# Transposes as products of column quarters with the identity, and one row a head of the row sums, in a two-layer graph network

## The chip, the cores and the metric

The kernel runs on one core of one Trainium2 chip. The metric is the device time of an execution in microseconds. The kernel before took 3508.07 us, the median of three runs (3501.76 to 3508.48).

## The reference

Sixteen graphs (B = 16) of N = 1024 nodes with D = 256 features are sent through two layers with one adjacency matrix a graph (int32, 1024 x 1024). All is f32. Cut to what matters:

```
h = relu(layernorm(x));  n = layernorm(h) * gamma1 + beta1            # layer 0
q = n as 8 heads of 32
a = softmax(where(adj > 0, q q^T / sqrt(32), -inf));  h = h + a q
h = h + gelu((layernorm(h) * gamma2 + beta2) W1 + b1) W2 + b2;  x = x + h
f = relu(layernorm(x));  u = f W                                       # layer 1
l = leaky_relu(u a_1 + (u a_2)^T + u a_12 u^T);  a = softmax(where(adj > 0, l, -9e15))
x = x + elu(f W_1 + (a f) W_2)
```

## The kernel before, in words

`fast_path` computes it when a bound on gamma1 and beta1 holds; `general_path` below it isn't entered here. Nodes lie on the 128 partitions in 8 tiles per graph (NT = 8), and each graph goes through these stages:

- `prologue` (lines 753 to 860) loads x, makes h and the values va, and its `turn` (796) transposes va into kT with features on partitions: 16 transposes of 128 x 128 per graph, four per call (two tiles of nodes, two groups of heads), into one PSUM tile `ptk` (801), copied by ScalarE (804).
- `attention` (931) has 32 units per graph: 2 halves of 512 queries, 2 groups of 4 heads (GH = 4), 8 key tiles. A unit makes `s`, the scores of four heads, in four row strips of the array (950, 32*128 in the profile), adds the mask on VectorE (971), takes exp on ScalarE (974), and a unit later `weigh` (982) makes `o` in four column strips, 32 columns a head (987). Sums of the exps are gathered by DMA (1011). `total` (896) turns them into `den` (901), where the sum of a head stands in all of that head's 32 rows, and copies it to `ds`.
- `finish` (914) transposes `ds` (row sums) and `os` (unnormalized outputs), four transposes each (922) into `ptds` and `ptos`, takes the reciprocal of one column a head of `ptds` (925), multiplies (927), and GpSimd adds it into h.
- `rest` (1074) has the feed-forward part and layer 1: `turn` (1107) transposes y into `pty` (1117); `expand` makes `ph` (1137), `contract` makes `po` (1160); `turn1` (1187) transposes the features into `ptf` (1193); `project` makes `puT`, `values` makes `pg`, `weights` the logits `lg`, read by VectorE (1241), `own` makes `pf`, and `attend` (1265) makes `pa`.

Those last products go through `matmul` (565): it cuts a product with 128 output rows into four with 32 columns of the stationary operand each ("quarters"), while the flag `quarters[0]` is set. The flag is cleared in `close_attention` (1048), after the last unit of attention, so that the last graph's rest of the work is on the whole array. The transposes don't go through it.

Graphs overlap: `stream_a` (attention of graph b), `stream_b` (rest of graph b - 1), `stream_c` (prologue of graph b + 1) and others are merged by places written out by hand (1446 to 1451), with a `clock` that counts planned us and `defer` for work that is due later. The order on each engine is fixed to the order of the program (1467 to 1476). Transposes are queued in `turns`, and `make_turns` (885) runs them ahead of a unit's scores, when there is room among three PSUM tiles (`psm`, tag `ps`): one tile for ptk, pty and ptf, two for finish. So a block of four transposes stands, mostly, after a quarter product or `o`, and before `s`. `setup` (660) transposes one weight once (672).

Of the kernel before, what the change touches and what calls it, by code (L numbers as in the profile page):

```python
# [9 lines left out]
F32 = mybir.dt.float32  # L10
# [6 lines left out]
P = 128  # L17
# [476 lines left out]
def fast_path(  # L494
# [28 lines left out]
    nc = tc.nc  # L523
    B, N, D = x.shape
    DFF = W1.shape[1]
    H, HD = 8, D // 8
    GH = 4
# [6 lines left out]
    TPH = QW // P  # L534
    CW = 256
    NCH = N // CW
    TPC = CW // P
# [3 lines left out]
    const = pool("const", 1)  # L541
# [16 lines left out]
    def ps_tile(shape, name, dtype=F32):  # L558
        return psm.tile(shape, dtype, tag="ps", name=name)
# [3 lines left out]
    quarters = [True]  # L563

    def matmul(out, lhsT, rhs, start=True, stop=True):
        if not quarters[0]:
            nc.tensor.matmul(out, lhsT, rhs, start=start, stop=stop)  # L567
            return
        for c in range(0, P, HD):
            nc.tensor.matmul(out[c : c + HD], lhsT[:, c : c + HD], rhs, start=start, stop=stop)  # L570

# [21 lines left out]

    ident = const.tile([P, P], F32, name="ident")
    make_identity(nc, ident)
    ident8 = const.tile([P, P], FP8, name="ident8")
    nc.vector.tensor_copy(ident8, ident, saturate=False)  # L600
    ones = const.tile([P, HD], F32, name="ones")
# [58 lines left out]
    def setup():  # L660
        wl, wa, wT, wb = (lp1.tile([P, DC, D], F32, tag="e1", name=f"stage_{i}") for i in range(4))
        weights_to_load.extend([(wl, W), (wa, a_12)])
        for t, src in rows_to_load:
            nc.sync.dma_start(t, src)
        for t, src in weights_to_load:
            nc.scalar.dma_start(t, src.rearrange("(c p) n -> p c n", p=P))
        yield

        for oc in range(DC):
            pt = ps_tile([P, DC, P], f"p_wT_{oc}")  # L670
            for ic in range(DC):
                nc.tensor.transpose(pt[:, ic, :], wl[:, ic, oc * P : (oc + 1) * P], ident)
            nc.scalar.copy(wT[:, oc, :], pt.rearrange("p c q -> p (c q)"))
        clock[0] += 0.5
        yield

        def product(dst, lhs, rhs, n, name):

            for oc in range(DC):
                pp = ps_tile([P, n], f"p_{name}_{oc}")  # L680
                for kc in range(DC):
                    matmul(
                        pp,
                        lhs[:, kc, oc * P : (oc + 1) * P],
                        rhs[:, kc, :n],
                        start=(kc == 0),
                        stop=(kc == DC - 1),
                    )
                nc.scalar.copy(dst[:, oc, :], pp)

        product(wb, wa, wT, D, "wb")
        clock[0] += 1.7
        yield
        product(wm, wT, wb, D, "wm")
        product(w_a2.unsqueeze(2), wT, a2c.unsqueeze(2), 1, "w_a2")
        product(wo2[:, :, D : D + 1], wT, a1c.unsqueeze(2), 1, "w_a1")
        nc.gpsimd.memset(wo2[:, :, D + 1 : D + 2], 0.0)
        clock[0] += 2.0
        yield


        sq = lp1.tile([P, DC * D], F32, tag="e1", name="sq")
        few = smallp.tile([P, 2 * DC], F32, tag="few", bufs=1, name="few")
        wmf = wm.rearrange("p c n -> p (c n)")
        nc.vector.tensor_tensor(sq, wmf, wmf, op=ALU.mult)
        nc.vector.tensor_tensor(few[:, :DC], w_a2, w_a2, op=ALU.mult)
        nc.vector.tensor_tensor(few[:, DC:], wo2[:, :, D], wo2[:, :, D], op=ALU.mult)
        nc.vector.tensor_reduce(seen[:, 0:1], sq, axis=mybir.AxisListType.X, op=ALU.add)
        nc.vector.tensor_reduce(seen[:, 1:2], few, axis=mybir.AxisListType.X, op=ALU.add)
        yield  # L710
# [25 lines left out]
    def defer(us, f):  # L736
        deferred.append((clock[0] + us, len(deferred), f))

        return clock[0] + us

    def run_deferred(until=0.0):
        while True:
            due = [d for d in deferred if d[0] <= max(until, clock[0])]
            if not due:
                return
            d = min(due, key=lambda d: d[:2])
            deferred.remove(d)
            d[2]()
# [4 lines left out]
    def prologue(b, st):  # L753
# [3 lines left out]
        va = st["va"] = vp.tile([P, NT, D], F32, tag="va", name=f"va_{b}")  # L757
# [38 lines left out]
        def turn(i):  # L796
            clock[0] += 0.5
            pt = ps_tile([P, NG, CW], f"ptk_{b}_{i}")
            for g in range(NG):
                for j in range(TPC):  # L800
                    nc.tensor.transpose(  # L801
                        pt[:, g, j * P : (j + 1) * P], va[:, i * TPC + j, g * P : (g + 1) * P], ident
                    )
            nc.scalar.copy(kT[:, :, i * CW : (i + 1) * CW], pt)

        steps = [
# [4 lines left out]
            value,  # L811
            lambda i: None,
            lambda i: turns.append((1, lambda: turn(i))),
        ]
        if b == 0:
# [25 lines left out]
            measure(1, "b")  # L841
            value(0)
            turn(0)
            convert(2)
            value(1)
            turn(1)
            convert(3)
            for f in (lambda i: measure(i, "a"), rectify, lambda i: measure(i, "b"), value):
# [65 lines left out]
    def finish(b, qh, g, ds, os):  # L914
        h = hs[b]
        finished[b, qh] = finished.get((b, qh), 0) + 1
        clock[0] += 1.0
        pts = []
        for n, c in (("ds", ds), ("os", os)):
            pt = ps_tile([P, TPH, P], f"pt{n}_{b}_{g}_{qh}")  # L920
            for t in range(TPH):
                nc.tensor.transpose(pt[:, t, :], c[:, t * P : (t + 1) * P], ident)  # L922
            pts.append(pt.rearrange("p t (j d) -> p t j d", d=HD))
        rl = smallp.tile([P, TPH, GH], F32, tag="rl", name=f"rl_{b}_{g}_{qh}")
        nc.vector.reciprocal(rl, pts[0][:, :, :, 0])
        ot = tmpp.tile([P, TPH, GH, HD], F32, tag="w2", bufs=3, name=f"ot_{b}_{g}_{qh}")
        nc.vector.tensor_mul(ot, pts[1], rl.unsqueeze(3).to_broadcast([P, TPH, GH, HD]))
        ho = h[qh][:, :, g * P : (g + 1) * P]
        nc.gpsimd.tensor_add(ho, ho, ot.rearrange("p t j d -> p t (j d)"))

# [143 lines left out]
    def rest(b, st, tails):  # L1074
# [10 lines left out]
        def add_residuals(t):  # L1085
            ht = h[t // TPH][:, t % TPH, :]
            nc.gpsimd.tensor_add(ht, ht, b2r)
            nc.gpsimd.tensor_add(xt[t], xt[t], ht)
# [4 lines left out]
        def ask(turn, c):  # L1093

            def f():
                clock[0] += 0.5
                turn(c)
                turned.add((turn, c))
            turns.append((1, f))
            if not quarters[0]:  # L1100
                make_turns()
# [5 lines left out]
        def turn(c):  # L1107
            if st["y", c][1] is not None:
                run_deferred(st["y", c][1])
            y = st["y", c][0]  # L1110
            for i in range(TPC):
                defer(4.0 * i + 2.0, lambda t=c * TPC + i: add_residuals(t))
            yT[c] = tmpp.tile([P, DC, CW], F32, tag="yT", name=f"yT_{b}_{c}")
            pt = ps_tile([P, DC, CW], f"pty_{b}_{c}")
            for dc in range(DC):
                for i in range(TPC):
                    nc.tensor.transpose(  # L1117
                        pt[:, dc, i * P : (i + 1) * P], y[:, i, dc * P : (dc + 1) * P], ident
                    )
            for dc in range(DC):  # L1120
                nc.vector.tensor_scalar(
                    yT[c][:, dc, :],
                    pt[:, dc, :],
                    g2[:, dc : dc + 1],
                    be2[:, dc : dc + 1],
                    op0=ALU.mult,
                    op1=ALU.add,
                )
# [46 lines left out]
        ft, ready1 = {}, {}  # L1175
# [11 lines left out]
        def turn1(c):  # L1187
            run_deferred(ready1[c])
            fT = st["fT"]
            pt = ps_tile([P, DC, CW], f"ptf_{b}_{c}")  # L1190
            for i in range(TPC):
                for dc in range(DC):
                    nc.tensor.transpose(  # L1193
                        pt[:, dc, i * P : (i + 1) * P], ft[c][:, i, dc * P : (dc + 1) * P], ident
                    )
            nc.scalar.activation(fT[:, :, c * CW : (c + 1) * CW], pt, AF.Relu)

        def project(qh, oc, fT, uT):
# [242 lines left out]
    def stream_s():  # L1441
        yield -0.3
        for i, _ in enumerate(setup()):
            yield 0.25 + 0.05 * i
# [3 lines left out]
    while any(p is not None for p in places):  # L1448
        i = min((p, i) for i, p in enumerate(places) if p is not None)[1]
# [92 lines left out]
```

## Time and profile before

| | |
|---|---|
| timed runs | 3508.48, 3508.07, 3501.76 us |
| the profiled execution | 3501.46 us, span 3499.6 us |
| TensorE clock granted | 0.998 |
| PE busy | 3445.0 us (98%), 46590 matmul records |
| DVE, ACT, POOL busy | 2758.3, 1857.8, 1412.8 us |
| transposes ptk, pty, ptf, ptds, ptos | 256 records each, 272 to 273 ns median length |
| who reads them | L804 ACT 576 ns, L1121 DVE 536 ns, L1196 ACT 597 ns, L925 DVE 248 ns, L927 DVE 692 ns (medians) |
| HBM read, written | 104.21 MB, 16.78 MB |

PE stands for TensorE's matmuls, PEld for its loads of the stationary operand, DVE for VectorE, ACT for ScalarE, POOL for GpSimd. In a group, "128*32 128x256" means 128 rows and 32 columns of the array, with 128 partitions of 256 elements streamed. Matmuls are pipelined: a record's length reaches from its start to its modelled end, and many records run side by side, so the sum of the means is no time; a group's busy time counts overlaps once. A group's last part is the idle time ahead of it, and who ended it.

### The profile page before, as it was taken

Reading aid. Unit: us, or ns where it says so; the run is one execution under the profiler, and the core shown is the slowest. Engines: PE = TensorE matmul, PEld = TensorE weight load, DVE = VectorE, ACT = ScalarE, POOL = GpSimd, SP = SyncE. Lnnn points to the kernel's source line nnn. Section 1 sums busy time; section 2 is a strip of 40 time slices with the busy share of each in tenths; the row PEclk is TensorE's granted clock in tenths of the full one; section 3 lists DMA queues with packets and bytes.
Section 4 is the critical chain, followed back from the end, with each engine's and each line's share of the span. In section 5 each row is a group of like instructions: output and inputs, shape, how many; then the busy total and the mean of one; then the engine's idle time right before and its main releaser. Section 6 shows DMA issues by size and latency. Waiting matters only on the chain.

```text
span 3499.6 us, 107320 instructions
## 1 busy us (share of the span) xinstructions
PE 3445.0 (98%) x46590; PEld 1673.9 (48%) x46590; DVE 2758.3 (79%) x5193; ACT 1857.8 (53%) x2184; POOL 1412.8 (40%) x1708
## 2 busy tenths in 40 slices
PE   6999999999999999999999999999999999999998
PEld 2244444444444444444444444444444444444477
DVE  6878788787877878888787888878878777887754
ACT  4555555555555555555555555555555555555522
POOL 3444443434434344343444534344344443434220
PEclk9999999999999999999999999999999999999999
DMA  7798889999899998989989899998989989899720
GB/s 183 147 182 173 181 164 185 182 186 188 161 187 176 191 184 165 181 167 190 195 167 183 165 185 185 177 190 164 186 177 191 183 165 179 171 191 182 147 63 14
DMA packets 281860, 597.81 MB, mean 171 GB/s; under 512 B 94882, under 2 KB 130084, under 8 KB 281380
## 3 DMA queue, kind: packets, MB, share of 16 engines
q0 software_dynamic: 124416, 453.04, 70.1%
q1 hardware_dynamic: 154276, 134.41, 15.5%
q8 instruction: 368, 6.03, 0.7%
q10 hardware_dynamic: 2688, 3.41, 0.3%
q14 instruction: 112, 0.92, 0.1%
HBM read 104.21 MB, written 16.78 MB: 35 GB/s over the span
## 4 chain that ended last, share of the span: by engine, by line
PE 94%; DVE 3%; DMA 1%; issue 1%; ACT 0%; POOL 0%; ACTq 0%; SPq 0%; DVEq 0%; POOLq 0%
PE s L950 15%; PE o L987 13%; PE pa L570 12%; PE po L570 12%; PE ph L570 12%; PE lg L570 10%; PE pg L570 3%; PE pf L570 3%; PE puT L570 3%; PE den L901 2%; PE ptf L1193 1%; PE pty L1117 1%; PE ptk L801 1%; PE ptos L922 1%; PE pa L567 1%
## 5 line engine op out<-in xcount | busy, mean ns | idle before, releaser
L974 ACT ACTIVATE e<-e 128x1024 f32<-128x1024 f32 x852 | 896.0, 1057 | 964.3 <-DVE e L971 728.3
L1011 POOL DMA_DIRECT2D acc<-e x864 | 754.9, 890 | 1438.3 <-DMA acc<-e 637.3
L971 DVE TENSOR_TENSOR e<-s,mk 128x1024 f32<-128x1024 f32 x852 | 1002.6, 1217 | 181.2 <-PE s L950 155.4
L950 PE MATMUL s<-kT 32*128 32x512 f32 x4096 | 592.5, 643 | 3.5 <-DVE odd L971 2.7
L987 PE MATMUL o<-e,va 128*32 128x512 f32 x3456 | 461.8, 605 | 2.1 <-ACT e L974 2.1
L570 PE MATMUL pa<-gw,e 128*32 128x258 f32 x7648 | 453.0, 380 | 0.0
L570 PE MATMUL lg<-fT,uT 128*32 128x256 f32 x7680 | 447.3, 379 | 0.0
L570 PE MATMUL ph<-yT,w 128*32 128x256 f32 x7808 | 446.5, 379 | 0.0
L570 PE MATMUL po<-w,hid 128*32 128x256 f32 x7680 | 439.3, 379 | 0.0
L570 PEld LDWEIGHTS ph<-yT,w 128*32 128x32 f32 x7808 | 255.3, 110 | 211.8 <-issue 51.1
L570 PEld LDWEIGHTS po<-w,hid 128*32 128x32 f32 x7680 | 250.3, 110 | 208.8 <-issue 58.3
L570 PEld LDWEIGHTS pa<-gw,e 128*32 128x32 f32 x7648 | 248.4, 110 | 212.0 <-issue 56.5
L570 PEld LDWEIGHTS lg<-fT,uT 128*32 128x32 f32 x7680 | 249.6, 110 | 209.0 <-issue 43.4
L1241 DVE SCALAR_TENSOR_TENSOR e<-lg,gw,mk 128x256 f32<-128x256 f32 x512 | 223.2, 477 | 72.0 <-PE lg L570 61.5
L1247 ACT ACTIVATE e<-e,shift 128x512 f32<-128x512 f32 x256 | 183.1, 717 | 181.6 <-DVE e L1246 116.0
L1144 DVE TENSOR_TENSOR hid<-ph,b1c 128x512 f32<-128x512 f32 x256 | 175.8, 687 | 91.6 <-PE ph L570 80.1
L950 PEld LDWEIGHTS s<-kT 32*128 32x128 f32 x4096 | 162.7, 184 | 163.8 <-issue 112.0
L987 PEld LDWEIGHTS o<-e,va 128*32 128x32 f32 x3456 | 68.6, 108 | 330.3 <-issue 187.3
L974 ACT ACTIVATE acc<-acc 128x1024 f32<-128x1024 f32 x124 | 131.1, 1057 | 132.9 <-DVE acc L971 128.4
L1246 DVE SCALAR_TENSOR_TENSOR e<-e 128x512 f32<-128x512 f32 x256 | 193.1, 754 | 8.8
L971 DVE TENSOR_TENSOR acc<-s,mk 128x1024 f32<-128x1024 f32 x124 | 146.1, 1218 | 20.2 <-PE s L950 19.8
L793 POOL TENSOR_TENSOR nrm<-nrm,g 128x256 f32<-128x256 f32 x128 | 112.9, 882 | 63.8 <-DVE nrm L727 63.8
(145 smaller groups left out, 3820.9 us busy)
## 6 DMA issues: line engine op xcount, KB each, us to landing
acc<-e POOLq DMA_DIRECT2D x864, 512.0 KB, 6.1
adj<-in_adj_dram SPq DMA_DIRECT2D x248, 256.0 KB, 5.6
h<-in_x_dram SPq DMA_DIRECT2D x64, 256.0 KB, 6.1
xb<-in_x_dram SPq DMA_DIRECT2D x128, 128.0 KB, 4.3
out_dram<-z SPq DMA_DIRECT2D x128, 128.0 KB, 4.0
adj<-in_adj_dram SPq DMA_DIRECT2D x4, 512.0 KB, 6.8
mk<-mq SPq DMA_TRANSPOSE x128, 6.5
w<-in_L_gnn_W_dram ACTq DMA_DIRECT2D x2, 1024.0 KB
```

The lines of the kernel that those rows point to most:

```text
L570: nc.tensor.matmul(out[c : c + HD], lhsT[:, c : c + HD], rhs, start=start, stop=stop)
L793: nc.gpsimd.tensor_mul(nrm, nrm, g1)
L901: nc.tensor.matmul(den[j * HD : (j + 1) * HD, :], ones, acc[j // 2][:, j % 2, :], start=acc is accs[0], stop=acc is accs[-1],)
L950: nc.tensor.matmul(sc[j // 2][:, j % 2, :], kT[r, g, kt * P : (kt + 1) * P], kT[r, g, qs], start=j >= by_pe, stop=True,)
L971: nc.vector.tensor_tensor(e, masked, mb, op=ALU.add)
L974: weights = lambda e=e, masked=masked: nc.scalar.activation(e, masked, AF.Exp, scale=SCALE)
L987: nc.tensor.matmul(o[j * HD : (j + 1) * HD, :], va[:, kt, (g * GH + j) * HD : (g * GH + j + 1) * HD], es[j // 2][:, j % 2, :], start=(kt = ...
L1011: nc.gpsimd.dma_start(sums[g, qh][i], e, accum_op=ALU.add)
L1144: nc.vector.tensor_tensor(hid[:, f0 : f0 + 2, :], ph, b1c[:, f0 : f0 + 2].unsqueeze(2).to_broadcast([P, 2, CW]), op=ALU.add,)
L1241: nc.vector.scalar_tensor_tensor(e[:, j, :], lg[:, j, :], gw[:, kt, D : D + 1], st[c // 2][:, kt // 2, qs, kt % 2], op0=ALU.add, op1=ALU.add,)
L1246: nc.vector.scalar_tensor_tensor(e, e, ALPHA, e, op0=ALU.mult, op1=ALU.max)
L1247: ready = defer(2.5, lambda: nc.scalar.activation(e, e, AF.Exp, bias=shift))
```

## The change

A new helper `transpose` sends each transpose as four products, while the quarters flag is set: the stationary operand is a quarter (32 columns) of the source, the moving one the identity, and the result goes to 32 partitions of the same PSUM tile. All five families and the weight's transpose in `setup` use it. With the flag cleared it is the transpose of before. For `ptds` the moving operand is `each_head`, four columns of the identity (one at every 32nd row), so that of the 128 rows of `ds` four are transposed, one a head; the PSUM tile is 128 x 4 x 4 instead of 128 x 4 x 128, and the reciprocal reads it whole. `each_head` is copied once by VectorE.

```diff
+    def transpose(out, src, columns=None):
+
+        if not quarters[0]:
+            nc.tensor.transpose(out, src, ident)
+            return
+        for c in range(0, P, HD):
+            nc.tensor.matmul(
+                out[c : c + HD], src[:, c : c + HD], ident if columns is None else columns, start=True, stop=True
+            )
...
+    each_head = const.tile([P, GH], F32, name="each_head")
+    nc.vector.tensor_copy(each_head, ident[:, ::HD])
...
-                nc.tensor.transpose(pt[:, ic, :], wl[:, ic, oc * P : (oc + 1) * P], ident)
+                transpose(pt[:, ic, :], wl[:, ic, oc * P : (oc + 1) * P])
...
-                    nc.tensor.transpose(
-                        pt[:, g, j * P : (j + 1) * P], va[:, i * TPC + j, g * P : (g + 1) * P], ident
-                    )
+                    transpose(pt[:, g, j * P : (j + 1) * P], va[:, i * TPC + j, g * P : (g + 1) * P])
...
-        for n, c in (("ds", ds), ("os", os)):
-            pt = ps_tile([P, TPH, P], f"pt{n}_{b}_{g}_{qh}")
+
+        for n, c, rhs in (("ds", ds, each_head), ("os", os, ident)):
+            pt = ps_tile([P, TPH, rhs.shape[1]], f"pt{n}_{b}_{g}_{qh}")
             for t in range(TPH):
-                nc.tensor.transpose(pt[:, t, :], c[:, t * P : (t + 1) * P], ident)
-            pts.append(pt.rearrange("p t (j d) -> p t j d", d=HD))
+                transpose(pt[:, t, :], c[:, t * P : (t + 1) * P], rhs)
+            pts.append(pt)
         rl = smallp.tile([P, TPH, GH], F32, tag="rl", name=f"rl_{b}_{g}_{qh}")
-        nc.vector.reciprocal(rl, pts[0][:, :, :, 0])
+        nc.vector.reciprocal(rl, pts[0])
         ot = tmpp.tile([P, TPH, GH, HD], F32, tag="w2", bufs=3, name=f"ot_{b}_{g}_{qh}")
-        nc.vector.tensor_mul(ot, pts[1], rl.unsqueeze(3).to_broadcast([P, TPH, GH, HD]))
+        os_t = pts[1].rearrange("p t (j d) -> p t j d", d=HD)
+        nc.vector.tensor_mul(ot, os_t, rl.unsqueeze(3).to_broadcast([P, TPH, GH, HD]))
```

In `turn` of the rest (pty) and `turn1` (ptf) the same replacement is made.

More of the change, by code (lines that the diff above doesn't have):

```diff
@@ L1116, in turn @@
                 for i in range(TPC):
-                    nc.tensor.transpose(
-                        pt[:, dc, i * P : (i + 1) * P], y[:, i, dc * P : (dc + 1) * P], ident
-                    )
+                    transpose(pt[:, dc, i * P : (i + 1) * P], y[:, i, dc * P : (dc + 1) * P])
             for dc in range(DC):
@@ L1192, in turn1 @@
                 for dc in range(DC):
-                    nc.tensor.transpose(
-                        pt[:, dc, i * P : (i + 1) * P], ft[c][:, i, dc * P : (dc + 1) * P], ident
-                    )
+                    transpose(pt[:, dc, i * P : (i + 1) * P], ft[c][:, i, dc * P : (dc + 1) * P])
             nc.scalar.activation(fT[:, :, c * CW : (c + 1) * CW], pt, AF.Relu)
```

## The prediction

> **What bounds the kernel now.** I read the page's shares and slices first, then the chain of work that ended last, then TensorE's groups with shapes kept apart, then the order of time around single blocks of transposes, and last what PE waits for.
>
> ```profile
> span 3499.6 us, 107320 instructions
> ...
> PE 3445.0 (98%) x46590; PEld 1673.9 (48%) x46590; DVE 2758.3 (79%) x5193; ACT 1857.8 (53%) x2184; POOL 1412.8 (40%) x1708
> ...
> PEclk9999999999999999999999999999999999999999
> ...
> PE 94%; DVE 3%; DMA 1%; issue 1%; ACT 0%; POOL 0%; ACTq 0%; SPq 0%; DVEq 0%; POOLq 0%
> ```
>
> TensorE is busy 98% of the span, at full clock, and 94% of the chain is PE. It stands idle for 3499.6 - 3445.0 = 54.6 us, about 22 us of that at the start. So an instruction stream on PE that gets longer or shorter by some ns moves the end by as much, unless it meets one of few waits.
>
> TensorE's groups, forms kept apart (count, then busy us and mean ns of one):
>
> ```profile
> L570 PE MATMUL ph<-yT,w 128*32 128x256 f32 x7808 | 446.5, 379 | 0.0
> ...
> L801 PE MATMUL ptk<-ident,va 128*128 128x128 f32 x256 | 43.7, 292 | 22.3 <-POOL va L794 22.2
> L1117 PE MATMUL pty<-ident,y 128*128 128x128 f32 x256 | 42.0, 286 | 0.3 <-DVE y L727 0.3
> L922 PE MATMUL ptds<-ident,ds 128*128 128x128 f32 x256 | 42.0, 286 | 0.0
> L1193 PE MATMUL ptf<-ident,ft 128*128 128x128 f32 x256 | 41.9, 286 | 0.9 <-DVE ft L727 0.9
> L922 PE MATMUL ptos<-ident,os 128*128 128x128 f32 x256 | 38.8, 274 | 3.4 <-DVE e L1241 3.4
> ```
>
> The five families are 1280 transposes (p_wT adds 4), one record each, on the whole array (128*128), together 208.4 us. The products run in column quarters (128*32), and an f32 product makes two records: po has 128 tiles x 8 sums x 4 quarters = 4096 products less the last, unquartered ones, but 7680 records. Means overlap, so prices must come from start to start. The order of time on PE around one block (start us, length us):
>
> ```profile
> 400.13 1.91 PE L570 MATMUL ph<-yT,w 128*32 128x256 f32 x32
> 401.86 3.64 PE L570 MATMUL po<-w,hid 128*32 128x256 f32 x64
> 405.42 0.66 PE L1117 MATMUL pty<-ident,y 128*128 128x128 f32 x4
> 406.01 1.14 PE L950 MATMUL s<-kT 32*128 32x512 f32 x8
> 407.08 1.07 PE L987 MATMUL o<-e,va 128*32 128x512 f32 x8
> 407.96 3.64 PE L570 MATMUL po<-w,hid 128*32 128x256 f32 x64
> 411.53 0.71 PE L950 MATMUL s<-kT 32*128 32x512 f32 x4
> ```
>
> Four quarter records start together (a quad). ph's 32 records are 8 quads in 401.86 - 400.13 = 1.73 us: 216 ns a quad of 256 columns. The first po's 16 quads (3.456 us) take 405.42 - 401.86 = 3.56 us up to pty: 0.11 us extra for leaving quarters. The second po runs to s, in rows of 32, without a block: 411.53 - 407.96 = 3.57 us, the same 0.11 us. So the block of four transposes costs just what lies between its start and that of s, 406.01 - 405.42 = 0.59 us; single records say 586 ns as the median of 176 such blocks: 164 + 109 + 109 + 203 ns.
>
> **The skill.** "TensorEngine Tiling (Array Packing)", Key Properties, says that a change of tiling mode drains the array: the trace agrees, 0.11 us at each change from quarters, above. Its Gotcha 2 says that column tiling excludes the transpose mode for f32; this trace has transposes as 128*128 alone, so it doesn't contradict, and it means that a quarter must be an ordinary, two-record product. "TensorE: Matmul & The Clock Gate", Part 4, gives some 275 ns for a transpose in context: the trace has 273 as the median, but that is length, and the next starts 109 ns later. The same page's Terms call the transpose mode four times faster for f32; here it is two: a product on the whole array (last rows, 128*128) takes 2 x 216 ns for 256 columns, half of it for 128, against 109. I use the trace's ratio.
>
> **The change, part by part.** The built program has the same order on every engine; each transpose is four quarter products in its place, and DVE gets one 128x4 copy. Nothing is moved past another queue, no DMA is added, the planner's costs are unchanged.
>
> *Price of a quad of 128 columns, Q.* No row shows it. From single record starts: 429 ns a quad of 512 columns (puT), 216 of 256, so 213 per 256 columns, and for 128 columns 216 - 107 = 109 ns. The floor is this:
>
> ```profile
> 73.00 0.43 PE L570 MATMUL p_w_a<-a1c,stage 128*32 128x1 f32 x32
> 73.36 0.66 PE L922 MATMUL ptds<-ident,ds 128*128 128x128 f32 x4
> 73.85 0.60 PE L922 MATMUL ptos<-ident,os 128*128 128x128 f32 x4
> ```
>
> Eight quads of one column, loads included, take 0.36 us with filling and drain; between, the quads start 31 to 32 ns apart, so four quarter loads don't hold a quad up for longer. Bounds of Q: 53 ns (half the streaming) and 131 ns (ph's loads show 255.3 us for 7808, 32.7 ns each, four in a row). I take 109.
>
> *A block of four (ptk, pty, ptf).* Before: 586 ns. After: four transposes x two records = 8 quads, 8 x 109 = 872 ns; the entry from quarters needs no drain, the exit to s pays the one that would have been paid anyway. +285 ns. Such blocks still in quarters: ptk 64, pty 62, ptf 60 (the last batch's tail stays as it was), 186 x 0.285 = +53.0 us. Where quarters follow rather than s (8 blocks, and p_wT), both drains go: 9 x 0.113 = -1.0 us.
>
> *finish (ptds, ptos), 64 times.* Before, by single records: 310 from the last quarter record to ds, 383 + 109 to os, 328 + 203 to s, less the 309 that quarters to s take without any block: 1.024 us. After: ds has 4 columns, 8 quads at the floor, 8 x 31.5 = 252 ns (bounds 31.5 and 109 a quad: 0.25 and 0.87 us); os 872, drain out as for the other blocks. Sum 1.124, +0.100 each, +6.4 us; three go on in quarters, -0.3 us.
>
> *The wait that ds covered.* What PE waits for has this line:
>
> ```profile
> PE ptos L922 <- DVE e L1241: 3.4, 14, 0.2
> ```
>
> In 14 of 64 finishes (one a batch) ptos starts 516 instead of 109 ns after the last ds record, since its PSUM slot is the one that DVE's L1241 is still reading. That release is set by DVE. Counted from the start of lg's last record, ptos could start at 310 + 383 + 109 = 802 ns today and does at 1209, when the slot is free: 407 ns lost. (The row's 3.4 us are less than 14 x 0.407 because the tail of ds counts as busy.) After the change ptos is reached at 196 + 252 = 448 ns, no drain and a short ds, and the slot still comes at 1209: 761 ns lost. Queued behind it on PE is the next unit's s, and all else. So what finish gained up to there is gone: 14 x 0.354 = +5.0 us. Bounds 0 (if DVE, with PE slower elsewhere, is earlier) and +12 (if the other 16 finishes behind lg begin to wait).
>
> *The rest.* ds's reciprocal now reads 16 elements side by side instead of strided; 64 x 248 ns on DVE (79% busy), at nothing: hidden beside PE; if not, some ns each. The each_head copy lies in DVE's 2.07 us of idle before the first x arrives, at nothing; without cover some 0.2 us once. At the start PE waits for POOL's va (22.2 us) at half speed, and the doubled records of the second ptk lie before the first s: +0.3 us. Readers of the longer blocks (ACT copies, DVE's yT) come 0.29 us later, beside the s and o that follow; their PSUM slots (3) are held as much longer: hidden, but 250 x 0.05 = +12 us if one time in six it isn't.
>
> Sum: 53.0 - 1.0 + 6.4 - 0.3 + 5.0 + 0.3 = +63 us. The profiled execution took 3501.46 us (span 3499.6 and 1.9 around it), so it would be 3564. Two of the three timed runs are at 3508, the third at 3502; from the median, 3508.07, the sum is 3571. I put the forecast between: 3568.
>
> **The rivals.** *Loads show.* A quad of 128 columns is short, and its loads no longer fit behind it: Q = 131, 250 blocks x 8 x 22 ns = +44, 3612 us. For it: loads are 110 ns long, longer than 109. Against: 31.5 ns a quad of one column, and whole-array transposes (loads of 141 ns) at 109. Half of it gives 3590. Chance 0.12.
>
> *Faster: one pass a record.* If a record against the identity streamed its 128 columns once (the f8 products at L570 start 215 ns apart for 512 columns, 54 for 128), Q = 54. The sum without the wait is 2000 x Q - 158.6 us (186 x 587 + 64 x 772 ns): it decides at Q = 79 ns, and Q = 54 gives -50, 3458 us. For it: only the speed of f8. Against: each f32 product in this trace runs at 216 for 256, whatever its operands. Chance 0.05.
>
> *A wash.* Q between, or blocks hidden behind DVE: only 32 us of PE idle after the start could take them in, and the blocks stand where PE waits for nothing. 3508, chance 0.03.
>
> **How the numbers follow.** The likeliest case has 0.80. Its own range: Q 105 to 113 is +-8, ds at 60 ns a quad +15, the wait -5 to +7, absorbed idle -8, base +-3.5; to the loads' half way up: 3548 to 3595. That leaves out half of the loads' case, the wash and the faster one, 0.14, and a little of the likeliest. About 0.2% (7 us) can be told from no change: faster 0.05, same 0.03, slower 0.92.
>
> **What would show it.** The profile after has 46590 + 250 x 28 (blocks with os) + 28 (p_wT) + 64 x 28 (ds) = 55410 PE records; pt groups as 128*32 with 272 ns mean; a block of four from its start to s 0.98 us (783 + 202), where it was 0.59; ptds 32 records in about 0.25 us up to ptos; PE's wait at ptos for DVE e nearer 10 us than 3.4; PE busy up by 55 to 60, DVE, ACT and POOL unchanged. Wrong it would be if the pty block takes under 0.75 us, or if PE's idle shrinks by the blocks' growth.

## The result, and the profile after

The changed kernel took 3571.27 us, the median of four runs (3564.97 to 3574.26), against 3508.28 us of the kernel before (3501.76 to 3509.41) in the same series: ratio 1.0185, 95% interval 1.0172 to 1.0198. It is 63 us slower; the sum of the prediction was +63 us and its forecast 3568 us. The profiled executions are 3501.46 and 3564.97 us, spans 3499.6 and 3563.2 us: +63.6 us.

From the page of the kernel after, the shares of the span and the chain that ended last:

```profile
span 3563.2 us, 124961 instructions
...
PE 3507.4 (98%) x55410; PEld 1792.8 (50%) x55410; DVE 2762.3 (78%) x5194; ACT 1860.8 (52%) x2184; POOL 1421.1 (40%) x1708
...
PE 94%; DVE 3%; DMA 2%; issue 1%; ACT 0%; POOL 0%; ACTq 0%; SPq 0%; POOLq 0%; DVEq 0%
```

PE is busy 62.4 us longer (55 to 60 were forecast) and has exactly the 55410 records that were counted; DVE, ACT and POOL moved by 3 to 8 us; PE's idle time is 55.8 us where it was 54.6. All but 1.2 us of the change is time in which PE is busy.

The groups of the transposes on PE, forms kept apart (count, then busy us and mean ns of one, then idle time before them):

```profile
L578 PE MATMUL ptos<-ident,os 128*32 128x128 f32 x2048 | 70.5, 275 | 7.8 <-DVE e L1250 7.8
L578 PE MATMUL ptk<-ident,va 128*32 128x128 f32 x2048 | 70.0, 277 | 21.0 <-POOL va L807 21.0
...
L578 PE MATMUL pty<-ident,y 128*32 128x128 f32 x1984 | 66.3, 273 | 0.0
L578 PE MATMUL ptf<-ident,ft 128*32 128x128 f32 x1920 | 63.8, 273 | 0.0
...
L578 PE MATMUL ptds<-each_head,ds 128*32 128x4 f32 x2048 | 29.7, 174 | 0.0
```

Four families went from 39 to 44 us busy to 64 to 71; only ptds fell, from 42.0 to 29.7. The same place in order of time, a pty block between po and s:

```profile
404.46 3.64 PE L570 MATMUL po<-w,hid 128*32 128x256 f32 x64
407.91 1.06 PE L578 MATMUL pty<-ident,y 128*32 128x128 f32 x32
408.90 1.14 PE L963 MATMUL s<-kT 32*128 32x512 f32 x8
```

po's 16 quads take 407.91 - 404.46 = 3.45 us, where they took 3.56: the drain in front of the block is gone. The block takes 408.90 - 407.91 = 0.99 us, where it took 0.59. Record by record, a quad of 128 columns starts 109 ns after the one before it in the median (ptf, pty, p_wT; 110 at the ninetieth percentile), and a block takes 985 to 987 ns from its start to s.

### The profile page after: what moved, and what is told of

It is laid out like the page before. It is cut to its first block, busy times and chain, and to the rows that moved or that the text cites. A ratio compares the mean times of both kernels' runs of the same rounds, so it can differ in the third digit from the quotient of the medians.

```text
span 3563.2 us, 124961 instructions
## 1 busy us (share of the span) xinstructions
PE 3507.4 (98%) x55410; PEld 1792.8 (50%) x55410; DVE 2762.3 (78%) x5194; ACT 1860.8 (52%) x2184; POOL 1421.1 (40%) x1708
## 4 chain that ended last, share of the span: by engine, by line
PE 94%; DVE 3%; DMA 2%; issue 1%; ACT 0%; POOL 0%; ACTq 0%; SPq 0%; POOLq 0%; DVEq 0%
PE s L963 15%; PE o L1000 13%; PE po L570 12%; PE ph L570 12%; PE pa L570 12%; PE lg L570 10%; PE pg L570 3%; PE pf L570 3%; PE puT L570 3%; PE ptos L578 2%; PE den L912 2%; PE pty L578 1%; PE ptf L578 1%; PE ptk L578 1%; DMA acc<-e 1%; PE pa L567 1%
```

## The experiments

Times of one series are compared with the kernel before in the same series. All kernels compute the reference in full.

**Every quad of 128 columns twice.** Each quarter product of ptk, pty, ptf, ptos and p_wT is made twice into the same place, those of ptds once. Does each quad cost its 109 ns of the end, or does something cover it?

```diff
-        for c in range(0, P, HD):
+        for _ in range(1 if columns is each_head else 2):
+            for c in range(0, P, HD):
...
```

> The changed kernel with every quarter product of ptk, pty, ptf, ptos and p_wT made twice into the same place (ds once). Theory (each quad of 128 columns costs 109 ns of the end, nothing covers it): 250 blocks x 8 quads x 0.109 = +218 us, 3789 us where the changed kernel runs at 3571, ratio to the kernel before 1.080. Rival (part of a block lies beside work of other engines that PE would have waited for): under +200 us. Rival (loads set the pace): the same cadence of 109 would have to appear with PEld's loads back to back; over +218.

Measured: 3785.29 us against 3505.81, ratio 1.0789 (1.0767 to 1.0811). The difference to the changed kernel's ratio is 0.0604 of 3506, or 212 us (203 to 221 with both intervals), for 218 expected. From its page:

```profile
PE 3729.2 (98%) x63442; PEld 2014.8 (53%) x63442; DVE 2750.0 (73%) x5194; ACT 1869.9 (49%) x2184; POOL 1405.8 (37%) x1708
```

PE is busy 222 us more than in the changed kernel. Blocks of quads lie on the path almost in full: the rival of covered blocks asked for less than 200 us, and at most some 15 of the 218 can be covered.

**What the loads allow.** The kernel before, with ds as a product on the whole array and four columns moving: two records a product, each with a load of 128 columns and next to nothing to stream.

```diff
-        if not quarters[0]:
+        if columns is None or columns is ident:
             nc.tensor.transpose(out, src, ident)
-            return
-        for c in range(0, P, HD):
-            nc.tensor.matmul(
-                out[c : c + HD], src[:, c : c + HD], ident if columns is None else columns, start=True, stop=True
-            )
+        else:
+            nc.tensor.matmul(out, src, columns, start=True, stop=True)
```

> ds is a product on the whole array with the four columns of the identity moving (two records of four columns each a product, loads of 128 columns), all else as in the kernel before. It measures what a load allows when nothing is streamed. If whole-array loads are hidden as well as quarter loads: some 32 to 55 ns a record, 8 records, a ds block of 0.31 to 0.5 us from its first record to os where it is 0.49: between -12 and 0 us, ratio 0.9965 to 1.000. If loads of 128 columns set the pace at their length (141 to 190 ns) or at the 109 ns of the transposes: 0.87 to 1.5 us, +24 to +65 us, ratio 1.007 to 1.019.

Measured: 3537.60 us against 3505.50, ratio 1.0085 (1.0064 to 1.0105). One finish in order of time:

```profile
230.91 1.05 PE L577 MATMUL ptds<-each_head,ds 128*128 128x4 f32 x8
231.83 0.63 PE L575 MATMUL ptos<-ident,os 128*128 128x128 f32 x4
232.39 1.14 PE L960 MATMUL s<-kT 32*128 32x512 f32 x8
```

Eight records take 231.83 - 230.91 = 0.92 us up to os, one each 112 ns by single records, though they stream only four columns: what is left to set this pace is the load of 128 columns. In quarters the same work, ptds of the changed kernel, runs at 32 ns a quad (median; mean 35), four loads and four product records in each. So the rival of "loads show" is excluded for quarters, and holds for the whole array. The transposes on the whole array, which load 128 columns too, start every 109 ns, close to these 112. So it isn't decided whether their streaming or their load sets their pace, and the prediction's ratio of two between an f32 product and a transpose may come from the load.

**The finish alone, and the order inside it.** In the first kernel ds and os are in quarters and ptk, pty, ptf are transposes as before; in the second all is as changed, but os goes ahead of ds.

```diff
-                    transpose(pt[:, g, j * P : (j + 1) * P], va[:, i * TPC + j, g * P : (g + 1) * P])
+                    nc.tensor.transpose(pt[:, g, j * P : (j + 1) * P], va[:, i * TPC + j, g * P : (g + 1) * P], ident)
...
```

> ds and os are made in quarters as in the changed kernel; ptk, pty and ptf are whole-array transposes. Theory: +0.100 x 64 for the longer finish and 14 x 0.35 for the uncovered wait: +11 us against the kernel before, ratio 1.003; so the 186 blocks of ptk, pty and ptf alone are the other 52 us of the change. Rival (blocks and finishes don't add, because the longer blocks shift DVE and so the slots): over 1.006 or under 1.001 here.

Measured: 3522.54 us against 3505.50, ratio 1.0043 (1.0027 to 1.0059): by the ratio +15 us (9 to 21) for +11 expected. Counted on PE from the last quarter record before a finish to s, the 64 finishes are 15.3 us longer than in the kernel before. So blocks and finishes add, and the blocks of ptk, pty and ptf are the other 48 us or so; counted in the same way they are 186 x 0.287 = 53.

```diff
-        for n, c, rhs in (("ds", ds, each_head), ("os", os, ident)):
+        for n, c, rhs in (("os", os, ident), ("ds", ds, each_head)):
...
-        nc.vector.reciprocal(rl, pts[0])
+        nc.vector.reciprocal(rl, pts[1])
```

> The changed kernel with os ahead of ds in a finish, so that ds takes the PSUM slot that DVE holds, and os's 872 ns lie ahead of it. Theory (the 14 waits are for that slot, and PE has nothing else to do meanwhile): a wait shrinks from some 730 to some 140 ns, 14 x 0.6 = -8 us against the changed kernel: 3563 where that runs at 3571, ratio to the kernel before 1.016. Rival (DVE is behind at those places anyway, and the next unit waits for it instead): no change, 1.0185.

Measured: 3565.26 us against 3505.50, ratio 1.0163 (1.0140 to 1.0185); expected 1.016. The interval touches that of the changed kernel, so the time alone doesn't prove it. The waits do. What PE waited for, first the line of the changed kernel, then the head of the list with os first:

```profile
PE ptos L578 <- DVE e L1250: 7.8, 14, 0.6
```

```profile
PE ptk L578 <- POOL va L807: 21.4, 3, 19.3
PE s L570 <- ACT acc L987: 6.7, 2, 4.6
PE s L963 <- DVE odd L984: 3.7, 2, 3.0
```

The 14 waits at the slot that VectorE reads (7.8 us as the row counts them, 730 ns each from record to record) are no longer in the list with os first. At these 14 places ds now starts 228 ns after os's last record, elsewhere 89, so some 140 ns of waiting are left, as worked out. Over the 64 finishes PE's records are 11.5 us shorter than in the changed kernel; against that stand 3.4 us of four waits for issue at lg and pf, which the changed kernel doesn't have. One finish that waits, in the kernel before and in the changed one:

```profile
338.68 0.66 PE L922 MATMUL ptds<-ident,ds 128*128 128x128 f32 x4
339.57 0.63 PE L922 MATMUL ptos<-ident,os 128*128 128x128 f32 x4 [0.23 <-DVE e L1241]
340.12 1.14 PE L950 MATMUL s<-kT 32*128 32x512 f32 x8
```


```profile
339.97 0.45 PE L578 MATMUL ptds<-each_head,ds 128*32 128x4 f32 x32
340.97 1.08 PE L578 MATMUL ptos<-ident,os 128*32 128x128 f32 x32 [0.55 <-DVE e L1250]
341.98 1.14 PE L963 MATMUL s<-kT 32*128 32x512 f32 x8
```

ds ends earlier and then PE stands until VectorE lets the slot go: from the start of ds to that of os it is 0.89 us before and 1.00 after, so a shorter ds gives nothing there.

**ds left as whole-array transposes, all else in quarters.** What does a change of array form in the middle of a finish cost?

```diff
-        for n, c, rhs in (("ds", ds, each_head), ("os", os, ident)):
+        for n, c, rhs in (("ds", ds, None), ("os", os, ident)):
...
-                transpose(pt[:, t, :], c[:, t * P : (t + 1) * P], rhs)
+                (transpose if rhs is not None else nc.tensor.transpose)(pt[:, t, :], c[:, t * P : (t + 1) * P], ident)
```

> The changed kernel with ds left as four whole-array transposes, all else in quarters. Theory with changes of array form: a finish enters the whole array for ds (310), 383, leaves it for os (203), then 785 + 202 to s: 1883 ns where it was 1333, +0.55 x 64 = +35 us, waits -1 us, blocks +52: +86 us against the kernel before, ratio 1.0245, slower than the changed kernel by 23 us. Rival without drains (only streaming counts): ds costs 436 where the quarters take 252, 64 x 0.18 = +12 us over the changed kernel, ratio 1.022.

Measured: 3583.66 us against 3505.81, ratio 1.0216 (1.0197 to 1.0235). That is 0.003 below the theory with drains, 1.0245, which the interval excludes, and at the rival's 1.022. The records, however, show each drain: 310 ns from the last quarter record to ds (196 in the changed kernel, where the form stays), 203 ns from the last ds record to os (109 between two transposes), and 1907 ns (median) from the last quarter record to s for 1883 expected. Over the 64 finishes PE's records are 34.8 us longer than in the kernel before, where the theory said 35, and 19.4 us longer than in the changed kernel. The profiled executions are 3584.6 - 3563.2 = 21.4 us apart, but they are the slowest of four runs and the fastest of four; by the medians it is only some 11 us. So the form changes are shown by the records, and why the medians show some 8 us less than their sum these runs don't tell.

**ds alone in quarters.** The part of the change that should gain.

```diff
-        if not quarters[0]:
+        if not quarters[0] or columns is None or columns is ident:
             nc.tensor.transpose(out, src, ident)
             return
...
```

> Only ds is made in quarters (four columns of the identity moving); ptk, pty, ptf, ptos and p_wT are whole-array transposes again. Theory (every piece of TensorE time counts from start to start, a change of array form costs its drain): a finish takes 196 + 7 x 31.5 + 20 to the last ds record, about 104 to the first os transpose, 383 + 203 to s, 1127 ns where it was 1333: -0.206 x 64 = -13.2 us; in the 14 finishes that wait for DVE's slot 0.26 us of it is lost again, +3.7. Sum -9.5 us against the kernel before: 3499 where that runs at 3508, ratio 0.997. Rival (DVE sets the pace around a finish, what ds saves turns into waiting in all of them): 3508, ratio 1.000, with PE's wait at ptos for DVE over 15 us.

Measured: 3504.95 us against 3505.50 over 14 and 19 runs, ratio 1.0000 (0.9986 to 1.0014). The gain isn't there, although the path of a finish is shorter: 1167 ns in the median where it is 1333 (1127 expected), and over the 64 finishes PE's records are 7.4 us shorter. The time is the rival's, but not its mechanism. It asked for over 15 us of waiting at ptos, and the line is that of the changed kernel:

```profile
PE ptos L575 <- DVE e L1248: 7.8, 14, 0.6
```

Nor did the variant with os first have the gain:

> As e_ds_only (only ds in quarters), with os ahead of ds. It asks whether the 9.5 us that e_ds_only should have gained and didn't lie at the 14 waits for DVE's slot. Theory: one change of form more a finish, 310 + 383 to the last os record, 203 to ds, 241, 104 to s, 1241 ns where the kernel before has 1333: -0.092 x 64 = -5.9 us, the 14 waits shorter than before by 0.09: -1.3; sum -7 us, ratio 0.998. If what e_ds_only lost lies elsewhere (gaps of some us on PE that come irregularly, and the half-speed clock after them), it shows no gain here either: 1.000.

Measured: 3507.18 us against 3503.60 over 22 and 27 runs, ratio 1.0005 (0.9998 to 1.0013). The 14 waits are not it: in this order PE waits 3.4 us for VectorE's slot, just as in the kernel before. What both kernels have in their runs is a lower granted clock of TensorE, 0.9959 and 0.9960 in the mean of all runs, where the kernel before has 0.9972 and 0.9975; 0.0014 of 3500 is 5 us. In the profiled executions the clock is at half in windows of mostly 3.4 or 6.8 us, and half of their length is lost: 17.6 and 16.2 us, 8.4 in the kernel before. Most of the windows follow a wait of PE of 1.6 to 5.7 us; at one (3138 us, ds alone) there are only two of 0.7 and 0.5 us, and at another (167 us, os first) none over 1 us. The profiled execution of ds alone, 3518.09 us, is 13 us above its kernel's median, so its delays are larger than usual. One window in it, all engines in order of time:

```profile
2703.72 0.86 POOL L1022 DMA_DIRECT2D acc<-e  x1 [8.36 <-DMA acc<-e]
...
2704.28 1.03 POOL L734 TENSOR_TENSOR rs_c<-ve_c,mhalf 128x2 f32<-128x2 f32 x1
2705.35 0.73 DVE L738 TENSOR_SCALAR y<-h,mv_c,rs_c 128x256 f32<-128x256 f32 x2 [5.29 <-POOL rs_c L734]
2706.00 2.34 DVE L982 TENSOR_TENSOR e<-s,mk 128x1024 f32<-128x1024 f32 x2
...
2707.27 3.20 PE L961 MATMUL s<-kT 32*128 32x512 f32 x8 [2.49 <-DVE e L982]
```

An adding DMA holds GpSimd for 8.36 us, GpSimd's rs_c holds VectorE for 5.29, and the mask addition queued behind it holds PE's next s for 2.49. The eight s records then last 3.20 us instead of 1.14: the second four start only when VectorE's second addition ends, and they are the first in a half-speed window that begins at 2708.3 us (1.06 to 1.21 us each, where the first four took 0.59 to 0.69). This place is shown. Why these kernels lose more to such gaps than the kernel before is not; that PE is now early enough to run into the others' delays is only argued, and stays open.

**A version without ds.** Since a quad of one or four columns costs 32 ns, the row sums can be made turned at once: summed exps stationary in quarters, one column of ones moving. Neither ds nor its transpose is needed.

```diff
-        den = ps_tile([P, QW], f"den_{b}_{g}_{qh}")
-        for j in range(GH):
-            for acc in accs:
-                nc.tensor.matmul(den[j * HD : (j + 1) * HD, :], ones, acc[j // 2][:, j % 2, :], ...)
-        ds = tmpp.tile([P, QW], F32, tag="w2", bufs=3, name=f"ds_{b}_{g}_{qh}")
-        nc.scalar.copy(ds, den)
+        den = ps_tile([P, TPH, GH], f"den_{b}_{g}_{qh}")
+        for t in range(TPH):
+            for j in range(GH):
+                for acc in accs:
+                    matmul(den[:, t, j : j + 1], acc[j // 2][:, j % 2, t * P : (t + 1) * P], ones[:, 0:1], ...)
+        ds = smallp.tile([P, TPH, GH], F32, tag="rl", name=f"rl_{b}_{g}_{qh}")
+        nc.vector.reciprocal(ds, den)
```

> The kernel before with the row sums made turned at once: den is 16 products a finish with quarters of the summed exps stationary and one column of ones moving, so that neither ds nor its transpose is needed, and finish transposes os alone. Theory: 32 quads x 31.5 = 1.01 us in place of two quads of 512 columns (0.86), finish 0.587 in place of 1.024 us: -0.29 x 64 = -18 us; the 14 waits go as finish takes one PSUM tile, -5.7; +0.6 in the first graph. -23 us: 3485 where the kernel before runs at 3508, ratio 0.993. Rival (instructions can't be supplied at 256 loads and products a microsecond, or loads of freshly summed exps stall): den takes 1.5 us or more, ratio 1.001 or above.

Measured: 3601.63 us against 3505.81, ratio 1.0274 (1.0254 to 1.0293), mean clock 0.987. The rival holds in its time and in its first cause, as the following shows, but not in its number for den. From the head of what PE waited for, and one place in order of time:

```profile
PE pa L570 <- issue: 23.9, 12, 3.1
...
PE ph L570 <- issue: 15.5, 7, 4.1
PE den L570 <- issue: 14.5, 7, 4.2
```

```profile
988.79 1.25 PE L570 MATMUL den<-ones,acc 128*32 128x1 f32 x128
989.92 1.07 PE L570 MATMUL pf<-wo,fT 128*32 128x256 f32 x16
990.78 1.03 PE L570 MATMUL pa<-gw,e 128*32 128x258 f32 x10
994.88 0.66 PE L570 MATMUL pa<-gw,e 128*32 128x258 f32 x4 [3.07 <-issue]
```

The burst itself is nearly as quick as expected (1.01 us): 128 product records, of 64 quarter products, and as many loads in 989.92 - 988.79 = 1.13 us, quads 33 ns apart (median). Two us later, in the middle of pa, PE stops for 3.07 us and waits for no semaphore. Such waits come to 66 us; the kernel before has none. In the trace's DMA records the queue named "instruction" brings packets of 16384 bytes, one in 9.5 us in the kernel before, and every one of these waits (28 over 0.4 us between 200 and 3450 us) ends 1.3 to 1.6 us after such a packet has landed; of moments taken evenly over that stretch 4% do. The Trainium skill ("Runtime: NRT & Kernel Launch", Instruction fetch mechanics) says that instructions are refilled in blocks of 16 KiB, 256 instructions, and that the cost is mostly hidden. The block size agrees, and so does the count: the 2 x 46590 loads and product records of PE in the kernel before make 364 blocks of 256, and 368 such packets came. Hidden the cost isn't where a burst uses up 256 in 1.1 us.

To test that, the same products in four parts, one a unit (the cut shows the main lines; while parts are left, `make_turns` also has room for one transpose block fewer):

```diff
+        if parts:
+            parts.pop(0)()
...
+        parts.extend(lambda t=t: part(t) for t in range(TPH))
```

> As e_den_turned (row sums made turned, no ds), but its 64 quarter products a finish are made in four parts, one a unit, 16 products or 8 quads each. The count of instructions is the same but for three reciprocals more a finish on DVE. Theory (e_den_turned lost its gain because 256 loads and products of one burst outran the supply of instructions, and TensorE then waited 1 to 4 us for the next 16 KB of them): spread out, waits for issue are under 8 us, the clock is back at 0.997, and the gain worked out for e_den_turned appears, -15 to -23 us against the kernel before: 3483 to 3491 where that runs at 3506. Rival (the mean rate is too high, or half-speed windows come from the small products themselves): waits for issue and the clock of 0.987 stay, ratio over 1.01.

Measured: 3668.69 us against 3503.60, ratio 1.0482 (1.0458 to 1.0505). The head of PE's waits, in part:

```profile
PE s L953 <- DVE e L974: 32.2, 29, 2.5
PE ph L570 <- DVE yT L1126: 24.1, 13, 3.4
...
PE pa L570 <- DVE rl L912: 11.8, 14, 0.9
```

The waits for issue fell from 66 to 8.5 us at nearly the same count of instructions, so the burst was their cause. But the version is slower still, and neither expectation held. The clock stays at 0.987: 15 of the 19 half-speed windows now follow waits for VectorE's e or yT. The row sums come three units later, `finish` with them, and the feed-forward part, which waits for both groups, leaves units of attention almost alone on PE. From 413.75 to 427.92 us four of them follow each other with only o, den and ptos between, and s waits for VectorE, 0.95 and 1.30 us at a time. From start to start s's records take 673 us, 587 in the kernel before, and each part's reciprocal makes PE wait for its slot (11.8 us at pa). How much of the loss belongs to the later sums, to the transposes that are held back, and to the reciprocals was not separated. No version that beats the kernel before was found.

## Why the prediction was right, point by point

- *PE's stream is the bound, start-to-start times are prices.* Shown by doubling the quads (212 of 218 us).
- *Q = 109 ns.* Measured 109. The step from 512 to 256 columns told it, and the quads of one column gave the floor. A transpose of 128 x 128 in quarters is two quads, a transpose on the whole array one record, and a quad and that record both take 109 ns.
- *A block +285 ns.* 0.986 us from start to s where it was 0.586, and 0.196 us from the last quarter record to the block where it was 0.310: +287 ns, +53 us as worked out.
- *A finish +100 ns.* Mis-sized. In the 50 finishes without the wait it takes 1508 ns (median) from the last quarter record to s, for 1433 worked out: ds takes 274 ns up to os where 252 were worked out, and os's last record starts 836 ns after its first, where it is 784 with os first. 50 x 75 ns are some 4 us too little in the sum.
- *The wait that ds covered, +5.0 us.* Right in place, count and cause: 14 waits, os starts 1208 ns after lg's last record where 1209 were taken, and such a finish grows by 453 ns (medians) where 454 were worked out.
- *Hidden parts at nothing.* ACT, DVE and POOL didn't come nearer to the bound; the readers of the longer blocks were never what PE waited for.
- *What was off.* The finish is some 4 us longer than worked out, and PE's idle time other than at ptos fell from 51.2 to 48.0 us, which the prediction had at nothing. That these two nearly cancel is luck. PE's busy time grew by 62.4 us, a little over the 55 to 60 forecast.
- *Rivals.* Loads that show: excluded in quarters (32 ns a quad of four columns). One pass a record, and the wash: excluded by Q and by the time. The 275 ns that the prediction takes from the Trainium skill ("TensorE: Matmul & The Clock Gate", Part 4) stand there beside a bf16 transpose, so their nearness to the f32 length of 273 shows nothing; the sum doesn't use them. That ds alone would gain followed from the same sum, and there the sum failed, by 7 to 10 us: it holds for PE's own time, and doesn't include what irregular gaps and the clock take.

## What to carry to other kernels

Price a replacement on a bound engine by start-to-start times, before and after it, in the stage where it stands; lengths and busy sums mislead when records overlap. A change of array form cost about 0.1 us each way here, so staying in one form pays only if what stays is not much longer: in a block of four transposes the second pass costs 4 x 109 = 436 ns, and what it avoids, one drain and the slow start of the first transpose, was 586 - 436 = 150. A gain of a few tenths of a per cent on one engine may not reach the end at all, when the others' delays and the clock lie in wait.

## What the runs showed of the hardware that was not expected

- On the whole array f32 products with four columns moving, each record with a load of 128 columns, start every 112 ns; four quarter loads of 32 columns with their products start every 32 ns.
- Bursts of 256 instructions in 1.1 us on TensorE were followed, about every second time and within some 7 us, by gaps of up to 4 us, 66 us in all, that end 1.3 to 1.6 us after a 16 KB block of instructions has landed. With 32 loads and 32 product records in 0.27 us (ptds) the changed kernel has no such wait; of the others with these bursts, those with the finish alone, os first, and the quads twice have 1.9 to 5.3 us.
- Windows at half clock begin mostly 1.5 to 5.3 us after the start of a wait of PE. Between 200 and 3450 us the kernel before has none, the one with the turned row sums 11, which lose 22 us. The length of a single wait doesn't decide it: a window of 6.8 us came with waits of 0.7 and 0.5 us (ds alone, 3138 us), and none with one of 3.31 us (the sums in parts, 372 us).
